# One output-projection tile for all heads, and one Q projection per chunk spread by way of DRAM

## The chip, the cores and the metric

The kernel runs on one core of one Trainium2 chip. The metric is the device time of one launch in microseconds (us). The profile is one execution of the program, recorded by the hardware profiler.

## What is computed

The input `x` has four images of 128 channels and 64 x 64 positions, so 4 x 4096 tokens of 128 channels. Two layers follow each other.

Layer 0 is self-attention with four heads of 32 channels over the 4096 tokens of each image, an output projection, the residual, and a normalisation over channels:

```
Q, K, V = split_heads(x @ Wq + bq), ... (x @ Wk + bk), ... (x @ Wv + bv)
attn = softmax(Q K^T * scale);  out = attn V
y = out @ Wo + bo + x
y = (y - mean) / sqrt(var + eps) * gamma + beta
```

Layer 1 takes that result and adds up three branches: a 3 x 3 convolution, a spectral branch (a channel mix in the Fourier domain, which this kernel rewrites as flips and small matrices), and a state-space branch (Mamba: projection, short convolution, SiLU, a scan over all tokens with 256 channels and 16 states, a gate, a projection).

## The kernel before

**Tiling.** A chunk is 512 tokens (`L`), so there are 32 chunks. A half `H` is one chunk with one pair of heads (`PAIRS` = 2); there are 64 halves. In a half the keys are walked in 32 pieces of 128 (`NT` = 32). The main loop counts steps `t`: step `H * 32 + m` works on piece `m` of half `H`. A chunk is therefore a slot of 64 steps (`SLOT`); below, "position" is the step within its slot.

**What every step does.** `scores_for_exp` (line 480) computes the scores of 128 keys against 512 queries for two heads: per head two matmuls for the high and low parts of Q, and one that subtracts the row maximum (`MX`, `sel`). The Scalar engine (ACT) exponentiates them (line 488). `scores_for_max` (line 436) works `LEAD` = 7 steps ahead for the next half's row maxima, which the Vector engine (DVE) reduces (line 443). `times_values` (line 500) multiplies the exponentials by V and adds up in the PSUM tile `po`; an extra column of ones gives the softmax sum. The two heads of a pair sit at partitions 0 to 32 and 64 to 96.

**The scan.** The state-space scan of an earlier chunk (two slots and 16 steps behind) runs beside that, one scan instruction in every even step: ACT makes the decays (line 801), the GpSimd engine (POOL) the input terms `db` (line 806), DVE scans (line 817), POOL multiplies and accumulates (lines 827 and 846).

**The side jobs.** All the rest is written as Python generators that a small planner, `Plan`, advances while the program is written. Nothing is decided at run time: each engine gets one fixed order. `plan.at(t, rank, job)` says from which step a job may begin. Each `yield` is a wait of at least one step; its letters name what the next piece takes: "P", "D" and "A" are places on TensorE, DVE and ACT, of which there are two each in odd steps and none (one for ACT) in even steps; "B" is one of two PSUM banks. Jobs of a lower rank number go first.

The side jobs that matter here:

- `project_q(H)` runs once per half: one matmul with 512 columns into a bank, then ACT writes the high part and DVE the low part of `Q` (lines 412, 417, 418). The weights hold each head's 32 columns twice, because the rows of `Q` are head 0 twice and head 1 twice (against the high and low parts of K).
- `project_kv` does the same for K, and K's parts already travel through DRAM (`kd`): stored on the SyncE queue (SP) and read back in `place_k`.
- `maxima(H)` turns the row maxima into a tile: POOL widens them (line 452), TensorE transposes (line 459).
- `normalise(H)` runs at positions 1 and 33. It sends the softmax sums through DRAM (`zd`, lines 518 and 521), takes the reciprocal on DVE (line 524), sends it back out (`rd`, line 526), reads it spread over partitions into `r` (line 530), and POOL multiplies the tile `oz[k]` by it (line 533). The tiles `oz[0]` and `oz[1]` have gaps of 32 rows, which hold zeros against zero rows of the projection weights.
- `output_projection(c)`, from position 9: ACT adds `bo` to the residual `xr` (line 548); then, for each of four groups of 128 tokens, two matmuls with `oz[0]` and `oz[1]` and one that adds the transposed residual through the identity matrix (lines 556 and 557), all into `py`; then statistics and the normalised tile `xh` (lines 564 to 587).
- `mamba_input(c)` waits for `xh`; from it come `scan_input`, `scan_bc`, `scan_dt` (which ends in three POOL multiplications, lines 739 to 741, for each of two channel halves), `spectral`, `convolve`, `gate` (lines 757 to 765) and, a slot later, `scan_output`, in which POOL gates the accumulators (line 938) before a projection (line 948).
- `scan_load` (line 784) brings the rows `B` and `C` of the scan over all partitions by DMA into a ring of three buffers, which POOL sets free.

Nearly all DMAs of the loop are issued by SP in one fixed order; a DMA whose data or buffer isn't ready holds up those behind it. The constants are loaded by DMAs that ACT issues before its first computation.

Of the kernel before, what the change touches and what calls it, by code (L numbers as in the profile page):

```python
# [155 lines left out]
def attention_then_conv_mamba(  # L156
# [41 lines left out]
    wat = const.tile([P, 1 + PAIRS, P], F32, name="wat_vo")  # L198
# [9 lines left out]
    Wo = [wat[:, 1 + k, :] for k in range(PAIRS)]  # L208

    wq_t = const.tile([P, PAIRS, 2, 2, HD], F32, name="wq_t")  # L210
    bq = const.tile([P, PAIRS], F32, name="bq")
    for h in range(HEADS):
        k, j = divmod(h, 2)
        c = COL["bq"] + h
        for r in range(2):
            nc.scalar.dma_start(wq_t[:, k, j, r, :], wq[h, :, j * HS : j * HS + HD])
            nc.scalar.dma_start(
                bq[j * HS + r * HD : j * HS + (r + 1) * HD, k : k + 1],
                vecs[j * HS : j * HS + HD, c : c + 1],
            )  # L220
    Wq = [wq_t[:, k].rearrange("c j r d -> c (j r d)") for k in range(PAIRS)]
# [6 lines left out]
    bvk = const.tile([P, PAIRS], F32, name="bvk")  # L228
    nc.vector.memset(wat[:, 1:, :], 0.0)
    nc.vector.memset(bvk, 0.0)  # L230
    for h in range(HEADS):
        row = h % 2 * HS
        hs = slice(h * HD, (h + 1) * HD)
        nc.scalar.dma_start(wat[row : row + HD, 1 + h // 2, :], wvo[1, hs, :])
        nc.scalar.dma_start(
            bvk[row : row + HD, h // 2 : h // 2 + 1], bv[0:1, hs].rearrange("o c -> c o")
        )
# [40 lines left out]
    def constants_of_the_rest():  # L278
# [25 lines left out]
        for k in range(PAIRS):  # L304
            nc.tensor.matmul(pb, Wo[k], bvk[:, k : k + 1], start=k == 0, stop=k == PAIRS - 1)
# [11 lines left out]

    oz = [const.tile([P, L], F32, name=f"oz{k}") for k in range(PAIRS)]
    for k in range(PAIRS):
        nc.gpsimd.memset(oz[k], 0.0)  # L320
# [84 lines left out]
    def project_q(H):  # L405
# [3 lines left out]
        yield ""  # L409
        bank = yield "PB"  # L410
        pq = bank_tile(bank, [P, L], f"pq_{H}")
        nc.tensor.matmul(pq, Wq[k], xqs[c], start=True, stop=True)
        yield "DA"
        plan.release(bank, 2)
        q = att.tile([P, 2, L], F32R, tag="Q", name=f"Q_{H}", bufs=3)
        bias = bq[:, k : k + 1]
        nc.scalar.activation(q[:, 1, :], pq, AF.Identity, bias=bias)
# [94 lines left out]
    def normalise(H, t0):  # L512
# [4 lines left out]
        for j in range(2):  # L517
            nc.sync.dma_start(zd[j : j + 1, :], oz[k][j * HS + HD : j * HS + HD + 1, :])
# [617 lines left out]
```

## Time and profile before

| | |
|---|---|
| median of the runs | 6233.53 us (6230.06 to 6236.76, 3 runs) |
| the profiled execution | 6236.14 us, of which 6234.4 us are its span |
| granted TensorE clock, mean over the span | 0.982 |
| first exponential's matmul starts | about 131 us into the span |
| last step of the main loop ends | about 5984 us |
| TensorE (PE) matmuls busy | 6005.2 us (96%) |
| TensorE weight loads (PEld) busy | 2540.9 us (41%) |
| POOL, DVE, ACT busy | 4579.0 us (73%), 4286.5 us (69%), 3585.0 us (58%) |
| DMA | 405 MB, mean 65 GB/s |

The busy share is of the whole span. Matmuls are pipelined and their ends are modelled, so the distance from one matmul's start to the next says more about TensorE than the length of a row. "Idle before" is the time that an engine stood still ahead of an instruction, and what ended it.

### The profile page before, as it was taken

What the parts mean: (1) busy time and instruction counts of PE and PEld (TensorE: products, weight loads), DVE (VectorE), ACT (ScalarE), POOL (GpSimd) and SP (SyncE); (2) the same over time, 40 slices, a digit from 0 to 9 for tenths busy, and PEclk for the clock granted to TensorE, in tenths of its full rate; (3) what the DMA queues carried; (4) which work ended last, traced back from release to release, by engine and by line L of the source; (5) the groups of instructions that cost most, each with busy time, mean ns of one, the idle gap of its engine ahead of it and who ended that gap; (6) DMA issues with size and microseconds to landing.
All of it is one profiled execution on the core that took longest, in us unless ns stands there. A gap on an engine that the chain in (4) does not pass through costs nothing. (4 is left out here: it accounts for less than half of the span.)

```text
span 6234.4 us, 83338 instructions
## 1 busy us (share of the span) xinstructions
PE 6005.2 (96%) x32076; PEld 2540.9 (41%) x32076; DVE 4286.5 (69%) x4406; ACT 3585.0 (58%) x4858; POOL 4579.0 (73%) x4819
## 2 busy tenths in 40 slices
PE   5999999999999999999999999999999999999966
PEld 2444444444444444444444444444444444444321
DVE  4556776777777676777667777776777666767647
ACT  1455666565666555666656566665566556556643
POOL 0005887778887777888787888777788777778877
PEclk7999999999999999999999999999999999999987
DMA  3001222223222222222322221122322211112223
GB/s 111 14 25 47 63 56 61 63 64 98 79 71 60 63 65 60 62 63 73 89 82 65 61 65 60 57 64 67 98 66 71 55 54 54 54 55 58 63 80 85
DMA packets 234624, 404.97 MB, mean 65 GB/s; under 512 B 39272, under 2 KB 40816, under 8 KB 234224
## 3 DMA queue, kind: packets, MB, share of 16 engines
q1 hardware_dynamic: 229840, 397.75, 22.6%
q8 instruction: 251, 4.11, 0.3%
q10 hardware_dynamic: 4384, 1.89, 0.1%
q14 instruction: 149, 1.22, 0.1%
HBM read 350.54 MB, written 49.02 MB: 64 GB/s over the span
## 5 line engine op out<-in xcount | busy, mean ns | idle before, releaser
L443 DVE TENSOR_REDUCE part<-s 128x2 f32<-128x1024 f32 x2048 | 2501.7, 1222 | 1627.4 <-PE s L436 1625.9
L488 ACT ACTIVATE e<-s 128x1024 f32<-128x1024 f32 x2048 | 2095.5, 1023 | 2271.7 <-PE s L480 2263.0
L500 PE MATMUL po<-e,V 128*33 128x512 f32 x8192 | 2160.9, 606 | 2.6 <-DVE oz L510 0.3
L480 PE MATMUL s<-Q,K 64*128 64x512 f32 x8192 | 1504.7, 445 | 22.3 <-ACT e L488 18.5
L436 PE MATMUL s<-K,Q 64*128 64x512 f32 x8192 | 1322.2, 400 | 41.2 <-DVE part L443 39.6
L827 POOL TENSOR_TENSOR hs<-hs,bc 128x512 f32<-128x512 f32 x952 | 1215.5, 1277 | 177.5 <-DVE hs L817 108.6
L480 PEld LDWEIGHTS s<-Q,K 64*128 64x128 f32 x8192 | 610.7, 185 | 1748.9 <-ACT e L488 1179.0
L806 POOL TENSOR_TENSOR db<-u,bc 128x512 f32<-128x512 f32 x948 | 1214.8, 1281 | 0.0
L846 POOL TENSOR_TENSOR acc<-acc,hs 128x512 f32<-128x512 f32 x900 | 1150.9, 1279 | 70.5
L817 DVE TENSOR_TENSOR_SCAN hs<-dA,state,db 128x512 f32<-128x512 f32 x832 | 1060.7, 1275 | 86.0 <-ACT dA L801 54.0
L436 PEld LDWEIGHTS s<-K,Q 64*128 64x128 f32 x8192 | 766.3, 186 | 276.7 <-DVE part L443 99.4
L480 PE MATMUL s<-MX,sel 64*128 64x512 f32 x4096 | 810.9, 392 | 0.0
L826 POOL COPY state<-hs 128x1 f32<-128x1 f32 x864 | 160.2, 185 | 844.8 <-DVE hs L817 844.8
L801 ACT ACTIVATE dA<-dt,negA 128x512 f32<-128x512 f32 x1024 | 702.6, 686 | 116.0 <-DVE hs L817 63.6
L500 PEld LDWEIGHTS po<-e,V 128*33 128x33 f32 x8192 | 299.3, 109 | 913.8 <-issue 879.7
L480 PEld LDWEIGHTS s<-MX,sel 64*128 64x128 f32 x4096 | 384.6, 185 | 92.6
L891 PE MATMUL pf<-xp,cw 128*128 128x512 f32 x576 | 288.2, 617 | 0.0
L452 POOL COPY wide<-mx 128x128 f32<-128x128 f32 x256 | 63.4, 294 | 200.7 <-DVE mx L449 200.7
L817 DVE TENSOR_TENSOR_SCAN hs<-dA,zero,db 128x512 f32<-128x512 f32 x128 | 163.2, 1275 | 7.7 <-POOL db L806 7.4
L840 PE MATMUL acc<-V,cst 128*128 128x512 f32 x128 | 90.1, 807 | 78.2 <-POOL V L827 78.0
L533 POOL TENSOR_TENSOR oz<-oz,rz 128x512 f32<-128x512 f32 x64 | 81.9, 1280 | 107.1 <-DMA rz<-rd 107.1
L891 PEld LDWEIGHTS pf<-xp,cw 128*128 128x128 f32 x576 | 96.2, 188 | 132.4 <-issue 127.4
(144 smaller groups left out, 3847.8 us busy)
## 6 DMA issues: line engine op xcount, KB each, us to landing
bc<-bcd SPq DMA_DIRECT2D x487, 512.0 KB
K<-kd SPq DMA_DIRECT2D x64, 256.0 KB
rz<-rd SPq DMA_DIRECT2D x128, 128.0 KB
K<-bcd SPq DMA_DIRECT2D x42, 256.0 KB
vd<-vst SPq DMA_DIRECT2D x32, 264.0 KB
V<-vd SPq DMA_DIRECT2D x32, 264.0 KB
xq<-in_x SPq DMA_DIRECT2D x32, 256.0 KB
xk<-in_x SPq DMA_DIRECT2D x32, 256.0 KB
```

The lines of the kernel that those rows point to most:

```text
L436: nc.tensor.matmul(sc[:, j, :], QT[H][rows[j], n, t * P : (t + 1) * P], KK[k][m][rows[j], :], start=n == 0, stop=n == 1,)
L443: nc.vector.tensor_reduce(part[H][:, t, :, m], sc, AX.X, ALU.max)
L480: nc.tensor.matmul(s[:, j, :], sel[rows[j], :] if n == 2 else KK[k][i][rows[j], t * P : (t + 1) * P], mov[rows[j], :], start=n == 0, stop= ...
L488: nc.scalar.activation(e, s, AF.Exp)
L500: nc.tensor.matmul(po[H][used[j], :], VA[i][:, t, 2 * k + j, :], e[:, j, :], start=m == 0, stop=m == NT - 1,)
L801: nc.scalar.activation(dA[c, v], dts[c][hf], AF.Exp, scale=negA[:, k : k + 1])
L806: engine.tensor_tensor(db[c, v], us[c][hf], bcs[c, n][0], ALU.mult)
L817: nc.vector.tensor_tensor_scan(hs, dA.pop((c, v)), db.pop((c, v)), state[:, k : k + 1] if c % NCH else zero, ALU.mult, ALU.add,)
L826: nc.gpsimd.tensor_copy(state[:, k : k + 1], hs[:, L - 1 :])
L827: nc.gpsimd.tensor_tensor(hs, hs, bcs[c, n][1], ALU.mult)
L846: nc.gpsimd.tensor_tensor(accs[c, hf], accs[c, hf], hs, ALU.add)
L891: nc.tensor.matmul(pf, cw[:, k, :], xps[c][:, dy : dy + RPC, dx : dx + W], start=k == 0, stop=False)
```

## The change

Two parts are rearranged.

**Q.** `project_q` runs once per chunk and computes all four heads with one matmul; ACT makes the high and DVE the low part, in the buffers that K's parts use. Both are stored to a DRAM tile `qd`. A new job, `place_q(H)`, reads from it, with four DMAs of 32 rows each, into the rows of `Q` of its half, 8 steps before the half's first row-maximum matmul. The weights and biases of Q are loaded once instead of twice.

**Output projection.** The two heads of a half are copied from `po` to a tile `oz[H]`; from there two more DMAs per half move them, without gaps, to their 32-row places in a tile `sums[c]` that holds all four heads of the chunk. The reciprocals are read into a tile of the same layout. After the second half, POOL multiplies once. `output_projection` is then one matmul with 512 columns and `Wo` as the stationary operand; DVE adds `bo` and the residual in one instruction and writes `xr`; four transposes bring it to the layout in which the statistics are taken. ACT's addition of `bo` is gone. The job starts three steps later and has two more planner stages.

Besides, `maxima` and `scan_output` wait one step more between POOL's work and the matmuls that read it, and the loads of Q's input and the projection of Q are placed earlier.

The diff, cut to its core:

```diff
-    wat = const.tile([P, 1 + PAIRS, P], F32, name="wat_vo")
+    wat = const.tile([P, 2, P], F32, name="wat_vo")
...
-        for r in range(2):
-            nc.scalar.dma_start(wq_t[:, k, j, r, :], wq[h, :, j * HS : j * HS + HD])
-            nc.scalar.dma_start(
-                bq[j * HS + r * HD : j * HS + (r + 1) * HD, k : k + 1],
-                vecs[j * HS : j * HS + HD, c : c + 1],
-            )
-    Wq = [wq_t[:, k].rearrange("c j r d -> c (j r d)") for k in range(PAIRS)]
+        nc.scalar.dma_start(wq_t[:, h, :], wq[h, :, j * HS : j * HS + HD])
+        nc.scalar.dma_start(
+            bq[h * HD : (h + 1) * HD, :], vecs[j * HS : j * HS + HD, c : c + 1]
+        )
+    Wq = wq_t.rearrange("c h d -> c (h d)")
...
-    for h in range(HEADS):
-        row = h % 2 * HS
-        hs = slice(h * HD, (h + 1) * HD)
-        nc.scalar.dma_start(wat[row : row + HD, 1 + h // 2, :], wvo[1, hs, :])
-        nc.scalar.dma_start(
-            bvk[row : row + HD, h // 2 : h // 2 + 1], bv[0:1, hs].rearrange("o c -> c o")
-        )
+    bvc = const.tile([P, 1], F32, name="bvc")
+    nc.scalar.dma_start(Wo, wvo[1])
+    nc.scalar.dma_start(bvc, bv.rearrange("o c -> c o"))
...
-    def project_q(H):
+    def project_q(c):
...
-        nc.tensor.matmul(pq, Wq[k], xqs[c], start=True, stop=True)
+        nc.tensor.matmul(pq, Wq, xqs[c], start=True, stop=True)
         yield "DA"
         plan.release(bank, 2)
+        hi = att.tile([P, L], F32R, tag="khi", name=f"qhi_{c}")
+        lo = att.tile([P, L], F32R, tag="klo", name=f"qlo_{c}")
+        nc.scalar.activation(hi, pq, AF.Identity, bias=bq)
+        nc.vector.scalar_tensor_tensor(lo, pq, bq, hi, ALU.add, ALU.subtract)
+        yield ""
+        qd[c] = dram.tile([2, HEADS, HD, L], F32, tag="qd", name=f"qd_{c}")
+        nc.sync.dma_start(qd[c][0].rearrange("h d l -> (h d) l"), lo.bitcast(F32))
+        nc.sync.dma_start(qd[c][1].rearrange("h d l -> (h d) l"), hi.bitcast(F32))
+
+    def place_q(H):
+        c, k = divmod(H, PAIRS)
+        while c not in qd:
+            yield ""
         q = att.tile([P, 2, L], F32R, tag="Q", name=f"Q_{H}", bufs=3)
-        bias = bq[:, k : k + 1]
-        nc.scalar.activation(q[:, 1, :], pq, AF.Identity, bias=bias)
-        nc.vector.scalar_tensor_tensor(q[:, 0, :], pq, bias, q[:, 1, :], ALU.add, ALU.subtract)
+        for j in range(2):
+            for r in range(2):
+                p0 = j * HS + r * HD
+                nc.sync.dma_start(
+                    q[p0 : p0 + HD].bitcast(F32), qd[c][:, 2 * k + j].rearrange("n d l -> d n l")
+                )
         QT[H] = q
...
# maxima, before its transposes
-        yield ""
-        yield ""
+        for _ in range(3):
+            yield ""
...
# times_values, last piece
-            nc.scalar.activation(oz[k][used[0], :], p[used[0], :], AF.Identity)
-            nc.vector.tensor_copy(oz[k][used[1], :], p[used[1], :])
+            oz[H] = att.tile([P, L], F32, tag="oz", name=f"oz_{H}", bufs=1)
+            nc.scalar.activation(oz[H][used[0], :], p[used[0], :], AF.Identity)
+            nc.vector.tensor_copy(oz[H][used[1], :], p[used[1], :])
...
# normalise
+            nc.sync.dma_start(zd[j : j + 1, :], o[j * HS + HD : j * HS + HD + 1, :])
+        for j in range(2):
+            nc.sync.dma_start(sums[c][head[j], :], o[j * HS : j * HS + HD, :])
...
-            nc.sync.dma_start(r[rows[j], :], rd[j : j + 1, :].to_broadcast([HS, L]))
-        yield ""
-        yield ""
-        nc.gpsimd.tensor_tensor(oz[k], oz[k], r, ALU.mult)
+            nc.sync.dma_start(inverse[c][head[j], :], rd[j : j + 1, :].to_broadcast([HD, L]))
         if k == PAIRS - 1:
-            plan.at(t0, 0, output_projection(H // PAIRS))
+            yield ""
+            yield ""
+            nc.gpsimd.tensor_tensor(sums[c], sums[c], inverse.pop(c), ALU.mult)
+            plan.at(t0, 0, output_projection(c))
...
# output_projection
-        yield "A"
-        nc.scalar.activation(xr, xr, AF.Identity, bias=bo)
+        bank = yield "PB"
+        pa = bank_tile(bank, [P, L], f"pa_{c}")
+        nc.tensor.matmul(pa, Wo, sums.pop(c), start=True, stop=True)
+        yield "D"
+        plan.release(bank, 2)
+        nc.vector.scalar_tensor_tensor(xr, pa, bo, xr, ALU.add, ALU.add)
         bank = yield "PB"
         py = bank_tile(bank, [P, TPC, P], f"py_{c}")
         for t in range(TPC):
-            if t == TPC // 2:
-                yield "P"
-            ts = slice(t * P, (t + 1) * P)
-            for k in range(PAIRS):
-                nc.tensor.matmul(py[:, t, :], oz[k][:, ts], Wo[k], start=k == 0, stop=False)
-            nc.tensor.matmul(py[:, t, :], xr[:, ts], ident, start=False, stop=True)
+            nc.tensor.transpose(py[:, t, :], xr[:, t * P : (t + 1) * P], ident)
...
# scan_output, before its matmuls
-        yield ""
-        yield ""
+        for _ in range(3):
+            yield ""
...
-            plan.at((H - 1) * NT - LEAD - 24, 0, load_q(H // PAIRS))
-        plan.at((H - 1) * NT - LEAD - 14, 0, project_q(H))
+            plan.at((H - 1) * NT - LEAD - 30, 0, load_q(H // PAIRS))
+            plan.at((H - 1) * NT - LEAD - 22, 0, project_q(H // PAIRS))
+        plan.at((H - 1) * NT - LEAD - 8, 0, place_q(H))
         plan.at(H * NT - LEAD, 0, maxima(H))
-        plan.at((H + 1) * NT + 1, 0, normalise(H, (H + 1) * NT + 9))
+        plan.at((H + 1) * NT + 1, 0, normalise(H, (H + 1) * NT + 12))
```

## Prediction

> **What bounds the kernel now.** I read the page first, then windows over single chunks, then TensorE's order of time inside them, and last the waits.
>
> ```profile
> span 6234.4 us, 83338 instructions
> PE 6005.2 (96%) x32076; PEld 2540.9 (41%) x32076; DVE 4286.5 (69%) x4406; ACT 3585.0 (58%) x4858; POOL 4579.0 (73%) x4819
> ```
>
> TensorE's row is full, but matmuls overlap in it, so it only names the suspect. Two whole chunks side by side, one from the middle and one from the last image:
>
> ```profile
> core 0: us, PE busy (x) PEld busy (x) DVE busy (x) ACT busy (x) POOL busy (x), PEclk, DMA share, GB/s
> 2852.64:3036.27 183.63, 182.95 (x1000) 78.16 (x999) 131.54 (x135) 111.43 (x152) 148.04 (x159) 1.00 0.33 95
> 5250.67:5437.70 187.03, 182.45 (x990) 76.20 (x988) 131.08 (x135) 111.38 (x151) 146.82 (x156) 1.00 0.19 55
> ```
>
> The columns after the window are its length and each engine's busy time. The clock is full. TensorE stands still for 0.7 us of 183.6 in the first, for 4.6 us in the second. No other engine is above 81%. Next, TensorE's own order, starts in the first column:
>
> ```profile
> 2879.60 0.73 PE L480 MATMUL s<-Q,K 64*128 64x512 f32 x4
> ...
> 2884.83 0.73 PE L480 MATMUL s<-Q,K 64*128 64x512 f32 x4
> ...
> 2887.17 0.73 PE L480 MATMUL s<-Q,K 64*128 64x512 f32 x4
> ...
> 2888.54 1.12 PE L412 MATMUL pq<-xq,wq_t 128*128 128x512 f32 x2
> ...
> 2890.58 0.73 PE L480 MATMUL s<-Q,K 64*128 64x512 f32 x4
> ...
> 2908.16 0.73 PE L480 MATMUL s<-Q,K 64*128 64x512 f32 x4
> ...
> 2909.53 0.66 PE L638 MATMUL pt<-cst,xh 128*128 128x128 f32 x4
> ...
> 2911.09 0.73 PE L480 MATMUL s<-Q,K 64*128 64x512 f32 x4
> ```
>
> Each L480 row opens a step, so the distance between two of them is a step's price. A bare step, 2884.83 to 2887.17, takes 2.34 to 2.36 us. The step with the output projection, 2879.60 to 2884.83, takes 5.23: the projection costs 2.87. The step with a Q projection, 2887.17 to 2890.58, takes 3.41: that matmul costs 1.06. The step with four transposes, 2908.16 to 2911.09, takes 2.93: they cost 0.57. Side work adds to TensorE's time in full, in odd steps, with nothing of it hidden.
>
> A rule of the Trainium skill speaks against counting on this: "Perfetto Trace Analysis", section "Identifying the Most-Contended Engine", holds matmul busy share to be a poor measure and wants weight-load share instead. That is 41% here, so by the rule TensorE has headroom, taking matmuls off it need not shorten anything, and the PE part of my sum would be nothing, with nothing to give back either: 6236.1 - 12 - 6 - 5, 2.6 less for the median, 6211 us. The step distances show the opposite, and I take them.
>
> **The change part by part.**
>
> *TensorE, per chunk.* Removed: two Q projections (2 x 1.055) and one output projection (2.87), 4.98 us. Added: one Q projection (1.055), the projection `pa`, which is of the same form (1.055), and four transposes of `xr` (0.573, as for `xh`): 2.68 us. The balance is -2.30 us, and over 32 chunks -73.5 us. For the transposes the page "TensorE: Matmul & The Clock Gate", section "Part 4: PE-mode transpose", gives about 275 ns each in a kernel, 1.10 us for four; then the balance would be -57 us. The trace has four of this very shape, at 0.57, and I use that.
>
> *The extra step in `maxima` and `scan_output`.* The waits that these can remove:
>
> ```profile
> PEld s L436 <- DVE part L443: 99.4, 126, 2.0
> PEld pm L459 <- POOL wide L452: 13.4, 35, 0.7
> PEld py L948 <- POOL acc L938: 13.2, 16, 2.6
> ```
>
> (total us, times, longest). One step is 2.35 us, more than the longest 0.7 of the first of POOL's two, so I take -12 of 13.4; of the second, whose waits reach 2.6, half: -6 (bounds 0 and -13). The row maxima come a step later, still some two steps before their first use at position 0 or 32.
>
> *Start.* ACT issues 42 constant DMAs, from 0.76 to 21.9 us, before its first computation at 21.98. Now there are 28 (four fewer for `wq_t` and for `bq`, three fewer for `Wo` and for `bv`). At 0.475 us from one issue to the next that is 6.7 us. Against it stands Q's pair of ACT and DVE instructions ahead of K's, with shared buffers. I take -5 (bounds -7 and +5). The `oz` memsets (1.0 us on POOL) go too; nothing waited for them.
>
> *ACT and DVE.* Per chunk ACT loses one Q part (0.68) and the `bo` addition (0.71). DVE loses one Q part (0.75) and gains the addition from `pa` (about 0.75). ACT is at 61% of a chunk; its loss is worth nothing. DVE's balance is nil. The 99.4 us in which row-maximum matmuls wait for DVE stay as they are; most of them sit at position 2, behind the copy of `po`, which is not touched. The later start (12 for 9) and the extra bank stage delay `xh` by about six steps, 14 us. What is late next is `scan_dt`, some 45 steps on; its last product `u` is finished near position 15, shortly before the scan of its chunk, so some of the planner's gaps between must shrink. I cost that at nothing, with 0 to +20 us in the range.
>
> *SP's queue.* Added per chunk: two stores of Q, eight loads, four moves of heads: 14 issues at about 0.4 us, 5.6 us of a queue that mostly waits. They move past one another thus: at positions 1 and 33 two moves stand ahead of the load of `zc` (+0.8 us for the sum's round trip; the reciprocal at 4 has had no idle time before it); at 17 and 49 four loads of Q follow `scan_load`, and K's loads and `wr` queue behind them (1.6 us, needed much later). Cover for `place_q` is eight steps, at position 17 about 21 us (steps of 2.34 with a gate, a transposition and a projection among them). The nearest rows: the rd to rz round trip holds SP 126.3 us in 64 waits, 2.0 us each; the slowest store in sight, `vd` in the crowded start, was issued at 28.91 and set ACT free at 39.8, 11 us. A load of 128 KB then lands 4 to 13 us after SP reaches it; either fits, so nothing. The moves of heads, SBUF to SBUF, have no row; 2 to 11 us by the same two, against five steps (12 us) before POOL needs them: nothing, +10 us at worst.
>
> *POOL.* One multiplication of 1.28 us per chunk goes, at position 39, where POOL has time. It does not go where POOL has none:
>
> ```profile
> 2893.89 1.28 POOL L827 TENSOR_TENSOR hs<-hs,bc 128x512 f32<-128x512 f32 x1
> 2895.24 1.29 POOL L846 TENSOR_TENSOR acc<-acc,hs 128x512 f32<-128x512 f32 x1
> 2896.49 1.27 POOL L806 TENSOR_TENSOR db<-u,bc 128x512 f32<-128x512 f32 x1
> ...
> 2897.99 1.27 DVE L817 TENSOR_TENSOR_SCAN hs<-dA,state,db 128x512 f32<-128x512 f32 x1
> ```
>
> From position 5 to 17 POOL runs without a gap: two bare steps give it 4.70 us, the scan takes 4.02 of them (3 x 1.28 and 0.18), and the six products of `scan_dt`, the gates and the last `oz` product come on top. TensorE's 2.87 and 1.06 us of side work in that stretch are what lets POOL keep up; the `db` above ends at 2897.76 and the scan that needs it starts 0.23 us later. Behind that scan on DVE stands the next row-maximum reduction, and for that TensorE waits. After the change the stretch holds one Q projection and `pa`, 2.11 us instead of 3.93, so 1.8 us less. Take off 0.23 and about 0.5 of slack on DVE, and 1.0 us per chunk comes back as a wait, in the 30 slots with a scan: +30 us. Bounds: 0 (if `scan_dt` falls beside other side work), and what the last image's chunks lose in their own first 46 us, where `scan_dt` falls in bare steps: 4.0 us by the windows, against 0.6 in the middle chunk, so +100.
>
> *Sum.* -73.5 - 12 - 6 - 5 + 30 = -66.5 against the profiled execution's 6236.1 (span 6234.4); that execution is 2.6 us above the median, so 6167 us. The tail after the last step (250 us) I leave as it is: `pa`, addition and transposes there (1.7, 0.75, 0.8) replace 5.3 us of `py`, and the wait of 18.3 us for the last `oz` stays; 5 us either way.
>
> **The rivals.**
>
> *Nothing is given back* (chance 0.25). `scan_dt` comes later and falls beside `pa`, the transposes and the gate's matmul. Then -96.5: 6137 us. For it: 19% of POOL is free over a chunk. Against it: the 0.23 us.
>
> *Most is given back* (0.19). POOL's and DVE's lag grows as in the last image, by some 2.7 us per chunk, 80 us: 6217 us. For it: the 187.03 us chunk, which lacks a K and V projection (2.1 us) and is still 3.4 us longer. Against it: `scan_dt` should come later, not earlier, than there.
>
> *Q arrives late* (0.08), the slower side. The loads of Q stand in SP's order behind `scan_load`, whose wait for POOL is SP's longest item (4041.6 us in 476 waits, the longest 37.0). If SP stood there for most of the 21 us, the first row-maximum matmul, and everything behind it on TensorE, would wait in each half. From 1.04 us per half on (66.5 / 64) the gain is gone; at 1.8 us it would be +115: 6282 us. Against it: at position 17 SP issued its `bc` load at 2899.28, one microsecond into the step.
>
> **How the numbers follow.** The likeliest case (0.48) spans 6150 to 6190 by its bounds. The range, 6122 to 6224, reaches to the first rival's lower end and takes in most of the second; outside are the third and the tails, about 0.18. This kernel's measurement can tell 0.2%, 12.5 us, from no change. Faster by more than that: 0.48 + 0.25 + two thirds of 0.19 = 0.86; within: 0.06; slower: 0.08.
>
> **What would show it.** Right: a middle chunk of about 182 us; steps with `pq` or `pa` at 3.4 us, with four `xr` transposes at 2.93; the wait of `pm` for `wide` near zero; 32 fewer POOL products; ACT's first computation near 15 us; more DVE scans waiting for POOL's `db`, with bare steps above 2.4 us near position 17. Wrong: waits of L436 for a DMA of Q (third rival); chunks still at 183 us with TensorE idle for 2 us or more in each (second); chunks below 181 us (first).

## The result and the profile after

The changed kernel takes 6134.17 us (median of 5 runs, 6132.92 to 6136.61) against 6233.53: a ratio of 0.984, 95% interval [0.9829, 0.9851], 99 us less. The prediction was 6167 us with 6122 to 6224 as its range; the direction and the range held, the middle was 33 us too high.

The page of the changed kernel, its span and the busy time of each engine:

```profile
span 6134.7 us, 82692 instructions
PE 5914.9 (96%) x31434; PEld 2454.4 (40%) x31434; DVE 4291.6 (70%) x4404; ACT 3557.2 (58%) x4794; POOL 4534.8 (74%) x4785
```

POOL has 34 instructions fewer. TensorE's share is the same 96% as before, which again says nothing about where the 99 us went. One chunk from the middle and one from the last image, as before (window and length, then the engines' busy time, the granted TensorE clock and the DMA columns):

```profile
2812.62:2994.45 181.83, 180.81 (x980) 75.56 (x978) 131.58 (x135) 110.90 (x150) 146.66 (x158) 1.00 0.37 104
5179.02:5359.67 180.65, 179.11 (x971) 74.17 (x970) 131.23 (x134) 109.58 (x148) 145.44 (x156) 1.00 0.24 65
```

The middle chunk lost 1.8 us (183.63 before). The chunk of the last image lost 6.4 (187.03 before); it had been the longer of the two and is now the shorter, as it should be, since it has no K and V projection (2.1 us). That second loss is what the prediction's sum did not hold.

TensorE's order of time in that middle chunk, three steps with the new side work (start, length, operation). As before, the distance from one `s<-Q,K` row to the next is the price of a step:

```profile
2825.53 0.73 PE L483 MATMUL s<-Q,K 64*128 64x512 f32 x4
...
2826.90 1.13 PE L397 MATMUL pq<-xq,wq_t 128*128 128x512 f32 x2
...
2828.94 0.73 PE L483 MATMUL s<-Q,K 64*128 64x512 f32 x4
```

```profile
2846.46 0.73 PE L483 MATMUL s<-Q,K 64*128 64x512 f32 x4
...
2847.84 1.13 PE L562 MATMUL pa<-op,wat_vo 128*128 128x512 f32 x2
...
2849.88 0.50 PE L483 MATMUL s<-Q,K 64*128 64x512 f32 x2
```

```profile
2856.93 0.73 PE L483 MATMUL s<-Q,K 64*128 64x512 f32 x4
...
2858.28 0.66 PE L569 MATMUL py<-cst,xr 128*128 128x128 f32 x4
...
2859.85 0.74 PE L483 MATMUL s<-Q,K 64*128 64x512 f32 x4
```

The steps take 3.41, 3.42 and 2.92 us; a bare one takes 2.35. So Q's projection and `pa` cost 1.06 us each and the four transposes 0.57, the prices of the prediction. The waits that it named, and two new ones, in the changed kernel (total us, times, longest):

```profile
PEld s L439 <- DVE part L446: 77.1, 125, 2.0
DVE hs L829 <- POOL db L818: 43.2, 57, 3.6
PEld s L483 <- DVE MX L470: 38.6, 29, 1.6
PE s L483 <- DVE MX L470: 25.9, 29, 1.1
```

Loads of weights for `pm` waited 13.4 us for `wide` before and wait 0.4 us now, and the second layer's `py` no longer waits for POOL's gate product. The wait for the row-maximum reduction on DVE fell from 99.4 to 77.1 us. DVE's scans wait for POOL's `db` more often, as forecast: 57 times, against 18 times before:

```profile
DVE hs L817 <- POOL db L806: 32.0, 18, 3.5
```

The last two lines of the view above are new. The tile of row maxima is late once per chunk, at position 32:

```profile
2897.32 0.74 PE L483 MATMUL s<-Q,K 64*128 64x512 f32 x4
2898.94 0.50 PE L483 MATMUL s<-MX,sel 64*128 64x512 f32 x2 [0.88 <-DVE MX L470]
```

Where the span's 99.7 us went, from the start of each chunk's first step in the two traces:

| stretch | before, us | after, us | difference | per chunk |
|---|---|---|---|---|
| up to the first exponential's matmul | 131.4 | 127.4 | -3.9 | |
| chunks 0 and 1 | 326.8 | 323.1 | -3.6 | -1.8 |
| chunks 2 and 3 | 369.6 | 359.9 | -9.7 | -4.9 |
| chunks 4 to 25 | 4050.2 | 4007.3 | -42.9 | -1.95 |
| chunks 26 to 30 | 934.0 | 903.4 | -30.6 | -6.1 |
| chunk 31 to its last step's start | 171.6 | 166.2 | -5.4 | -5.4 |
| after that | 250.9 | 247.5 | -3.4 | |

### The profile page after: what moved, and what is told of

Read it like the earlier page. It is cut to its first block, busy times and chain, and to the rows that moved or that the text cites. A ratio compares the mean times of both kernels' runs of the same rounds, so it can differ in the third digit from the quotient of the medians.

```text
span 6134.7 us, 82692 instructions
## 1 busy us (share of the span) xinstructions
PE 5914.9 (96%) x31434; PEld 2454.4 (40%) x31434; DVE 4291.6 (70%) x4404; ACT 3557.2 (58%) x4794; POOL 4534.8 (74%) x4785
## 5 line engine op out<-in xcount | busy, mean ns | idle before, releaser
L439 PEld LDWEIGHTS s<-K,Q 64*128 64x128 f32 x8192 | 762.0, 185 | 255.2 <-DVE part L446 77.1
L701 POOL TENSOR_TENSOR xs<-xs,sg_x 128x512 f32<-128x512 f32 x64 | 82.4, 1287 | 59.1 <-ACT sg_x L625 59.1
```

The costliest lines, as they stand in the source:

```text
L439: nc.tensor.matmul(sc[:, j, :], QT[H][rows[j], n, t * P : (t + 1) * P], KK[k][m][rows[j], :], start=n == 0, stop=n == 1,)
```

## The experiments

The theory on trial: TensorE's prices hold, so its saving is 2.30 us per chunk; what a kernel gains beyond or short of that depends on where the planner then puts POOL's side products against the scan and against the matmuls that read them. The rival: the removed work and the removed waits are worth a fixed amount each, wherever the rest stands. Each kernel was timed in alternation with the kernel before, whose medians there were 6231 to 6234.5 us.

From here on, a chunk or a position without a number is a mean: of chunks 4 to 25 for the middle chunks, of chunks 26 to 30 for the last image. "In the written order" means the step in which the planner hands an instruction to its engine; an engine that is behind runs it some steps later.

### One part at a time

The kernel before with the Q part alone:

```diff
-    def project_q(H):
+    def project_q(c):
...
+    def place_q(H):
...
-            plan.at((H - 1) * NT - LEAD - 24, 0, load_q(H // PAIRS))
-        plan.at((H - 1) * NT - LEAD - 14, 0, project_q(H))
+            plan.at((H - 1) * NT - LEAD - 30, 0, load_q(H // PAIRS))
+            plan.at((H - 1) * NT - LEAD - 22, 0, project_q(H // PAIRS))
+        plan.at((H - 1) * NT - LEAD - 8, 0, place_q(H))
```

> The kernel before with the Q part of the change alone (one Q projection per chunk, its parts stored to qd and placed 8 steps ahead; eight constant DMAs fewer); output projection, its position 9 and the two-step waits as before. Theory A (each matmul taken off TensorE is paid back in full, and the parts add up): one 1.06 us projection less in each of 32 chunks is -34 us, and eight ACT issues of 0.475 us less at the start is -4, so about 38 us below the kernel before, ratio 0.994. Theory B (most of the 99 us comes from where the side jobs fall, not from TensorE's work): the last image's chunks, 187 us each in the kernel before, may move by several us, either way, so the total leaves -38 by more than 10.

Measured: 6275.03 us, 1.0061 [1.0045, 1.0078]. It is slower by 40 us with 34 us less on TensorE. Its middle chunks take 187.7 us (184.1 before). With Q's second projection gone, both halves of `scan_dt` come due together, and in the written order POOL gets all six of its products at position 1 (three at 5 and three at 11 before). It runs them in the steps at positions 3 to 5. POOL's rows in chunk 15 (start, length), and below them two of DVE and one of TensorE:

```profile
2898.80 1.27 POOL L754 TENSOR_TENSOR spe<-u,spe 128x512 f32<-128x512 f32 x1
2900.16 1.29 POOL L755 TENSOR_TENSOR dt<-dt,spe 128x512 f32<-128x512 f32 x1
2901.52 1.27 POOL L756 TENSOR_TENSOR u<-dt,xs 128x512 f32<-128x512 f32 x1
2902.75 1.29 POOL L754 TENSOR_TENSOR spe<-u,spe 128x512 f32<-128x512 f32 x1
2904.12 1.28 POOL L755 TENSOR_TENSOR dt<-dt,spe 128x512 f32<-128x512 f32 x1
2905.48 1.29 POOL L756 TENSOR_TENSOR u<-dt,xs 128x512 f32<-128x512 f32 x1
...
2909.57 1.27 POOL L821 TENSOR_TENSOR db<-u,bc 128x512 f32<-128x512 f32 x1
```

```profile
2910.87 1.28 DVE L832 TENSOR_TENSOR_SCAN hs<-dA,state,db 128x512 f32<-128x512 f32 x1 [2.46 <-POOL db L821]
2912.07 1.20 DVE L458 TENSOR_REDUCE part<-s 128x2 f32<-128x1024 f32 x1
...
2913.33 0.73 PE L451 MATMUL s<-K,Q 64*128 64x512 f32 x4 [0.48 <-DVE part L458]
```

Read from the top: 8 us of products hold up `db`; the DVE scan stands 2.46 us for `db`; the reduction queued behind that scan starts late; TensorE waits for it. Positions 6, 8 and 10 take 2.74, 3.19 and 3.17 us and not 2.38, 2.39 and 2.48 as before. This is the mechanism of the prediction's POOL step, at twice its price, but not in the changed kernel. It is 1.9 us of some 5 us of new waits in a middle chunk: the rest stands at position 15 (0.9, a wait for DVE's reduction), 21 (1.2, a wait for POOL's gate product) and 33 to 35 (1.0, DVE's reduction again). In the last image the same edit parts the six products, three at 61 and three at 5: positions 6, 8 and 10 fall from 3.78, 3.04 and 3.19 us to 2.35, 2.45 and 2.48, and the chunk from 186.8 to 182.3.

The kernel before with the projection part alone:

```diff
-        nc.gpsimd.tensor_tensor(oz[k], oz[k], r, ALU.mult)
...
+            nc.gpsimd.tensor_tensor(sums[c], sums[c], inverse.pop(c), ALU.mult)
...
+        nc.tensor.matmul(pa, Wo, sums.pop(c), start=True, stop=True)
...
-        plan.at((H + 1) * NT + 1, 0, normalise(H, (H + 1) * NT + 9))
+        plan.at((H + 1) * NT + 1, 0, normalise(H, (H + 1) * NT + 12))
```

> The kernel before with the output-projection part alone (all heads moved into one tile, one long matmul, addition on DVE, four transposes, start at position 12; six constant DMAs fewer); Q as before, two-step waits as before. Theory A: 2.87 - 1.06 - 0.57 = 1.24 us per chunk, -40 us, and -3 at the start: 43 us below the kernel before. Theory B: since this part also starts the chain towards the next scan some six steps later, the last image's chunks lose their stalls as well (187 to about 182 us, five or six chunks, -25 to -30): about 70 us below the kernel before.

Measured: 6172.6 us, 0.9899 [0.9884, 0.9914]: 61 us less, of which TensorE's balance is 40 (1.24 us per chunk). This lies between the two theories. Middle chunks take 183.4 us, those of the last image 181.3 (186.8 before). All of the surplus is in the last image: 5.5 us per chunk there, 1.1 in chunks 2 to 25. There the written order gives POOL the six products at 5 and 9 and no longer all at 1, and positions 6, 8 and 10 take 2.38, 2.34 and 2.48 us.

The kernel before with its projection started later and nothing else:

```diff
-        plan.at((H + 1) * NT + 1, 0, normalise(H, (H + 1) * NT + 9))
+        plan.at((H + 1) * NT + 1, 0, normalise(H, (H + 1) * NT + 15))
```

> The kernel before with one number changed: the output projection may start at position 15 instead of 9, so that the chain behind it comes about six steps later, as in the changed kernel; no work is removed. Theory A (the last image's stalls go because TensorE, ACT and POOL have less to do): the last image's chunks stay near 187 us and the time within 10 us of the kernel before. Theory B (they go because scan_dt's six POOL products no longer fall in bare steps): the last image's chunks come down to 182 to 183 us and the kernel gains about 25 to 30 us, middle chunks unchanged at 183.6.

Measured: 6302.04 us, 1.0105 [1.009, 1.012], slower by 68; neither theory had that. In the last image the edit doesn't move the six products, which stay at position 1 with 3.76, 3.03 and 3.19 us at 6, 8 and 10, so theory B isn't tested by it. In the middle chunks the projection's 2.87 us of matmuls stood at position 11, beside POOL's busy stretch, and lengthened its steps. Moved to 17, they leave bare steps there, and positions 14 to 16 stretch by 2.4 us together. In chunk 14 TensorE waits 2.73 us for an exponential of ACT; ahead of it on ACT stands an instruction that waits 3.34 us for POOL's gate product `zg`. So a start that is only later is not what helped.

The changed kernel with its projection started where it was before:

```diff
-        plan.at((H + 1) * NT + 1, 0, normalise(H, (H + 1) * NT + 12))
+        plan.at((H + 1) * NT + 1, 0, normalise(H, (H + 1) * NT + 9))
```

> The changed kernel with one number set back: the output projection may start at position 9 instead of 12. By the written order the middle chunks keep scan_dt's products in two places (1 and 9), but the last image's chunks get all six at position 1, as the kernel before had them. Theory C: the last image's chunks go from 180.7 to 184 to 186 us, six or seven of them, +20 to +35 us; middle chunks within 1 us. Rival (the last image gains because TensorE has less to do): last image's chunks stay near 181, time within 10 us of the changed kernel.

Measured: 6314.81 us, 1.0132 [1.0117, 1.0147], 181 us above the changed kernel, far above both theories. TensorE's wait for the sums, a single one of 21.3 us in the changed kernel, is here (total us, times, longest):

```profile
PE pa L562 <- POOL op L547: 129.9, 30, 22.1
```

In its middle chunks the step with `pa`, position 9, takes 8.3 us and not 3.4: POOL's product of the sums stands behind the scan's products and `scan_dt`'s. In the changed kernel the matmul stands at position 13, and in the loop it waits for nothing. The later start belongs to the one long matmul.

### Is it POOL?

The Q part alone, with `scan_dt` started four steps later, so that its six products split:

```diff
-            plan.now(1, scan_dt(c, hf, xd))
+            plan.at(plan.t + 4, 1, scan_dt(c, hf, xd))
```

> The Q part alone, as in e1, with one edit: scan_dt may begin four steps after scan_bc instead of at once. By the written order that moves the six POOL products of scan_dt in a middle chunk from one place (all six at position 1) to two places (three at position 3, three at 9); the last image's chunks keep theirs, three at 61 and three at 5. Theory C (e1 lost its gain because both halves of scan_dt fell on POOL together, in bare steps): middle chunks fall from 188.0 us to 182 to 184, and the kernel from 1.006 of the kernel before to 0.993 to 0.997, that is, the 34 us of TensorE work come out. Rival D (it is the place of the Q projection, or SP's extra DMAs, which are as in e1): no more than 10 us below e1.

Measured: 6245.17 us, 1.0018 [1.0009, 1.0027], 30 less than the Q part alone. That is more than rival D allows and less than theory C had (6190 to 6215). Positions 6, 8 and 10 go back to 2.35, 2.44 and 2.53 us, as C says. Positions 15 and 21 get somewhat worse (3.62 and 5.91 us, from 3.22 and 5.51).

The Q part alone, in the same order of work, without two of the three products of each half (this leaves out both subtractions of `scan_dt`, so its step sizes are other numbers):

```diff
-        nc.gpsimd.tensor_tensor(e, w, e, ALU.subtract)
-        nc.gpsimd.tensor_tensor(z, z, e, ALU.subtract)
```

> The Q part alone, as in e1, with two of scan_dt's three POOL products left out in each half (spe and the subtraction from dt; the step sizes dt are then not quite softplus). Order and places are those of e1; POOL has 4 x 1.28 us less in each chunk, at the place where six stood together; TensorE, DVE and ACT keep all they have. Theory C (POOL is what TensorE waits for there): most of the 4 to 5 us per chunk go, 30 chunks, so 100 us or more below e1. Rival E (ACT's and DVE's part of scan_dt, or the scan's own order on DVE, holds TensorE): under 30 us below e1.

Measured: 6227.01 us, 0.9988 [0.998, 0.9997], 48 less than the Q part alone. Neither number came (100 or more, less than 30). Positions 6, 8 and 10 take 2.35, 2.35 and 2.45 us. Nothing but work on POOL was taken away, so the 2.0 us per chunk at these positions were POOL's. Positions 15 (3.20) and 21 (5.51) do not move: those are other waits, which theory C had counted in.

### The third steps

The changed kernel with `maxima` back at two steps:

```diff
 # maxima, before its transposes
-        for _ in range(3):
-            yield ""
+        yield ""
+        yield ""
```

> The changed kernel with the wait in maxima set back from three steps to two. Theory A: the third step makes the tile of row maxima late in each half at position 32 (that step takes 3.49 us in the changed kernel, 25.9 us of TensorE waits for MX in 29 halves), so going back removes about 26 us and brings back at most the 13 us of waits for the widened maxima: 13 to 26 us below the changed kernel. Rival: the maxima tile is late for another reason (its bank is given late), then the waits for MX stay and 0 to 13 us come on top.

Measured: 6122.3 us, 0.9816 [0.9802, 0.9831]. It beats both kernels, the changed one by 12 us. Position 32 falls from 3.49 to 2.67 us; loads of weights for `pm` wait for `wide` again, 20.0 us in 39 waits (0.4 in the changed kernel). In this order of work the third step costs more than it saves. It is not alone in that: position 32 still stands 0.3 us over a bare step, so a part of the rival holds too, as the next experiment shows.

The changed kernel with `scan_output` back at two steps:

```diff
 # scan_output, before its matmuls
-        for _ in range(3):
-            yield ""
+        yield ""
+        yield ""
```

> The changed kernel with scan_output back at two steps, all else kept: its matmul goes from position 23 to 21, four steps after POOL gets the gate product. Theory A (the third step takes a wait away, as the prediction's -12 and -6 said it would): position 21 is 5.5 us and not 4.27, 32 x 1.26 = +40, so 6174; at the prediction's size (0.19 us a chunk) 6140. Theory B (in the changed kernel POOL is in time at position 21 too, since its sums products stand elsewhere): 6128 to 6140, position 21 at 4.3.

Measured: 6206.75 us, 0.9958 [0.9944, 0.9973]: 73 us above the changed kernel, well over what either theory gave the step. Position 21 takes 7.1 us in the middle chunks, where its work is worth 4.27. In chunk 15, POOL's gate product, then TensorE:

```profile
2896.37 2.48 POOL L950 TENSOR_TENSOR acc<-acc,zg 128x512 f32<-128x512 f32 x2
```

```profile
2894.22 0.73 PE L483 MATMUL s<-Q,K 64*128 64x512 f32 x4
...
2897.68 3.55 PE L960 MATMUL py<-acc,outw 128*128 128x512 f32 x4 [2.02 <-POOL acc L950]
...
2902.14 0.50 PE L483 MATMUL s<-Q,K 64*128 64x512 f32 x2
```

TensorE stands 2.02 us for the first of two products and stretches the matmuls over the second: this step takes 7.92 us. The same two rows in the changed kernel:

```profile
2869.04 2.51 POOL L950 TENSOR_TENSOR acc<-acc,zg 128x512 f32<-128x512 f32 x2
```

```profile
2873.02 1.98 PE L960 MATMUL py<-acc,outw 128*128 128x512 f32 x4
```

POOL ends at 2871.55, TensorE comes at 2873.02 and waits for nothing. POOL is no faster; the matmul stands two positions later. The matmuls of position 21 there would have come at about 2868.3 (the step starts at 2866.92, side work 1.37 us into it) and would have waited until 2870.3, the end of the first product, as they do here; that is an estimate. In the last image of this experiment, the planner also put the six `scan_dt` products together, and positions 6, 8 and 10 take 2.71, 3.03 and 3.21 us there. By whole chunks the loss is 2.3 us, in chunks 2 to 25 as in the last image, for position 32 gives 1.15 us back: it takes 2.34 us here, with the third step of `maxima` in place. With `scan_output`'s matmul at position 21 a bank is free two steps sooner, POOL widens the maxima at position 27 and not at 29, and the tile is in time. So the late tile of the changed kernel has two causes, the third step of `maxima` and the bank that `scan_output`'s third step holds longer.

Both back at two steps:

```diff
 # maxima and scan_output, in each
-        for _ in range(3):
-            yield ""
+        yield ""
+        yield ""
```

> The changed kernel with maxima and scan_output both at two steps: the one long matmul and the single Q projection as they are. The maxima's third step cost 12 us (e4). The planner then also puts POOL's six scan_dt products of a last-image chunk together at position 1. Theory A (the third step of scan_output is needed, and six products in a row cost 2 us a chunk as in e1): 6134 - 12 + 40 + 5 x 2 = 6172. Theory B (the removed PE work is all there is): 6122 to 6130.

Measured: 6168.14 us, 0.9897 [0.9882, 0.9912]. Theory A's number, but not by its parts: position 21 takes 4.77 us here, 0.5 over its work and not 3. Another 1.1 us per chunk are at positions 33 to 37, where two multiplications of the convolution stand ahead of a row-maximum reduction on DVE. Taking a step away in one job has moved others.

The kernel before with the Q part and both third steps:

```diff
 # the Q part as above; maxima and scan_output, in each
-        yield ""
-        yield ""
+        for _ in range(3):
+            yield ""
```

> The Q part alone (as e1) with both third steps of the change added: scan_output's matmul then stands at position 23 of a chunk and not 21, the maxima's turn goes to 28. In e1 (6275) position 21 took 5.53 us where its work is priced at 4.27, and POOL's six products at position 1 cost 2.05 us at positions 6 to 10; they stay there. Theory A (the gate product on POOL is what position 21 waited for; moving away from it pays): position 23 takes 4.27, some 24 middle chunks x 1.26 = -30, the maxima's third step gives up to 10 back: 6245 to 6255. Theory B (POOL is behind by a fixed amount of work, so the wait only turns up at another position): 6265 or more, with a new step that is over its price by about as much.

Measured: 6253.62 us, 1.0033 [1.0021, 1.0046], 21 us less than the Q part alone, as theory A had it. The step with the second layer's output matmuls, now at position 23, takes 4.27 us; positions 8 and 10 stay at 3.2.

The changed kernel without its Q part:

```diff
-    def project_q(c):
+    def project_q(H):
...
-            plan.at((H - 1) * NT - LEAD - 30, 0, load_q(H // PAIRS))
-            plan.at((H - 1) * NT - LEAD - 22, 0, project_q(H // PAIRS))
-        plan.at((H - 1) * NT - LEAD - 8, 0, place_q(H))
+            plan.at((H - 1) * NT - LEAD - 24, 0, load_q(H // PAIRS))
+        plan.at((H - 1) * NT - LEAD - 14, 0, project_q(H))
```

> The changed kernel without its Q part: one long projection and both third steps, but Q projected once for each half as before. Added back is one 1.055 us projection a chunk, 34 us. By itself the Q part made the kernel before 40 us slower (e1). Theory A (what the Q part is worth depends on where it lets the planner put POOL's work; beside the other parts the places are good and its TensorE price holds or more): 6168 to 6190. Theory B (the Q part costs in any company, through its two copies by DRAM and its earlier start): 6134 or less. With the projection alone and two steps at 6172.6 (e2), and the maxima's third step at 12, the sum of parts would be 6185.

Measured: 6151.42 us, 0.9869 [0.9852, 0.9885]. This is below theory A's bounds and above B's. The two third steps are worth 21 us here (against the projection alone, 6172.6) and 34 in the changed kernel (against both at two steps); the Q part then brings 17 of TensorE's 34. The 21 us are those of `maxima`: `scan_output`'s matmuls stand at position 25 in both kernels. With the projection alone `pm` waits for `wide`,

```profile
PE pm L446 <- POOL wide L439: 21.4, 26, 1.6
```

and positions 29 (where it stands) and 30 take 7.3 us together. Here it stands at 30, one wait of 0.8 us is left, the two positions take 5.9 us, and position 32 takes 2.45. The step that costs 12 us in the changed kernel gains 21 in this one.

### How late Q may be placed

The changed kernel with two steps between `place_q` and Q's first use, not eight:

```diff
-        plan.at((H - 1) * NT - LEAD - 8, 0, place_q(H))
+        plan.at((H - 1) * NT - LEAD - 2, 0, place_q(H))
```

> The changed kernel with Q placed 2 steps ahead of its first use instead of 8, about 5 us instead of 21; all else in the same order. The prediction's two bounds for the landing after SP reaches the loads were 4 and 13 us (four issues of 0.4 us included). If 4: nothing, within 5 us of the changed kernel. If 13: TensorE waits some 8 us for Q in each half and loses part of that, 300 us or more slower. What lies between gives the landing time: the wait per half is the landing less about 5 us.

Measured: 6599.01 us, 1.0588 [1.0573, 1.0604], 465 us above the changed kernel, 7.3 us per half. One of the waits in its chunk 15, first SP's issue of a `bc` load and of the four loads of Q, then TensorE:

```profile
3086.47 0.37 SPq L796 DMA_DIRECT2D bc<-bcd  x1
3086.89 1.87 SPq L419 DMA_DIRECT2D Q<-qd  x4
```

```profile
3094.47 2.00 PE L439 MATMUL s<-K,Q 64*128 64x512 f32 x4 [8.19 <-DMA Q<-qd]
3096.40 1.92 PE L503 MATMUL po<-e,V 128*33 128x512 f32 x4
3098.25 1.22 PE L483 MATMUL s<-Q,K 64*128 64x512 f32 x4
```

Q is there 7.6 us after SP begins to issue. The loads were due in the step that starts at 3078.68, but SP stood 10.7 us at the `bc` load ahead of them, waiting for POOL to set its buffer free, and issued them when TensorE had been waiting for 0.6 us. This is the mechanism of the prediction's third rival. In the changed kernel SP issued the loads of the same half at 2859.36, within the step at position 17, and the first matmul that needs them follows in the step at 2878.27 (position 25). With the 7.6 us of this experiment that leaves about 12 us to spare, an estimate; the trace of the changed kernel has no wait of TensorE for Q.

## Why the prediction came out as it did

**TensorE, -73.5.** The prices were right: 1.06, 1.06 and 0.57 us in the three steps above. The rule that the prediction set aside (the Trainium skill, "Perfetto Trace Analysis", section "Identifying the Most-Contended Engine") names two measures of TensorE's headroom, the share of peak arithmetic and the share of weight loads. The prediction had taken the second alone; by itself PEld's 41% would be room to spare, and the result speaks against that here. The first was not worked out. For the transposes the prediction multiplied a duration. The Trainium skill ("TensorE: Matmul & The Clock Gate", section "Part 4: PE-mode transpose") gives about 275 ns for one of bf16 in one kernel, and an f32 transpose lasts about that here (the maxima's, in the changed kernel: count, total busy us, mean ns of one):

```profile
L462 PE MATMUL pm<-cst,wide 128*128 128x128 f32 x256 | 42.4, 289 | 0.0
```

But four of them overlap, and add 0.57 us to a step, not 1.1.

The prices hold for work that is alone in its step; work in company costs less. The two `pdt` matmuls took one step of 4.27 us at position 63 before, so 1.92 us together; now they stand apart and cost 1.05 each. The transposes of the second row maxima cost 0.39 us beside convolution matmuls (a step of 4.65 us, and 4.26 without them), and 0.58 alone at position 60 now. So a middle chunk has 1.9 us less work on TensorE in the new order, not 2.30.

**The middle chunks, by errors that cancel.** By the prediction's terms a chunk gains 2.30 + 18/32 - 30/32 = 1.93 us on average. Chunks 4 to 25 gained 1.95. That the two agree is luck. TensorE's term was 0.4 too large, as just said, and three others were wrong:

- *POOL gives back 1.0 us per chunk.* It did not. Bare steps near position 17 stayed at 2.35 but for position 16 (2.44 before, 2.54 after), position 21 stands 0.2 over a bare step, and positions 6 and 10 take 0.16 less together. More scans wait for `db`, but the steps there do not lengthen. The step that failed took `scan_dt` to stay inside the stretch while the side work left it, 2.11 us of 3.93. In chunk 15 the steps at 5 to 17 have 3.75 us of side work: `pq` at 5, a gate's matmul at 9 and `pa` at 13 (1.06 each), and the transposes of `xr` at 17 (0.57); with the gate's matmul at 17 they had 4.99 before. And the planner put half of the products at position 1, ahead of the stretch and beside a `pdt` matmul that stands there now, and half at 9, behind the gate's matmul. Which of the two kept the wait away is not shown. That the forecast mechanism exists is shown by the Q part alone: with all six at position 1 it cost 1.9 us per chunk.
- *The third step of `maxima`, -12.* The wait of `pm` went, as said. "Still some two steps before their first use" was wrong: once per chunk the tile is late at position 32, by 1.14 us, and going back to two steps made the kernel 12 us faster. The prediction counted the wait that a step takes away, and not the slack that it uses up at the other end. Nor did it see that POOL's widening itself would come two steps later, at position 29 and not at 27, for want of a bank; where it stays at 27, as with `scan_output` back at two steps, the third step makes nothing late.
- *The waits for DVE stay as they are.* Position 2, where most of them sat, fell from 3.10 to 2.39 us in the middle chunks, and the waits at 0 and 30 by 0.3 each: a `pdt` matmul now stands in the step before position 2, and the maxima's transposes at 30 and not at 27. In all fourteen traces position 2 takes 2.35 to 2.4 us where position 1 has side work, and 3.1 to 3.2 where it has none.

**The third step of `scan_output`, -6.** Read from a trace in which, in the written order of the middle chunks, TensorE's matmuls stood at position 31, five behind POOL's gate product at 26, so that nearly nothing waited. In the changed order the product stands at 18 and the matmuls three positions behind it with two steps, five with three. Taking the step back costs 73 us there, by the experiment, the jobs that move with it included. It was a large part of the gain rather than a small addition to it; not all of it, since with both third steps taken back 65 of the 99 us are left.

**Where the other 33 us came from.** Chunks 2 and 3 and 26 to 31 gained 45.7 us; at the predicted 1.93 us each it would have been 15.4. That is 30 of the 33; the tail has the rest. Chunk 3 and those of the last image had, before, what the Q part alone has in its middle chunks: six `scan_dt` products in bare steps. Of the 6.1 us per chunk of the last image, TensorE's work in its new company is 2.5; 2.8 are the stalls at positions 6, 8 and 10 (3.78, 3.04 and 3.19 us before; 2.35, 2.45 and 2.44 after), 0.9 the one at 15, 1.0 those at 33 to 35, 0.6 those at 21 and 30; the maxima's late tile takes 1.1 back, and position 27 another 0.4 (these parts add up to 6.3). The prediction saw these stalls, in the 187.03 us chunk, and used them as an upper bound of the loss. It did not ask whether the change would take them away: there the products now stand at 3 and 9. Where an experiment on the changed kernel puts all six back at position 1 (`scan_output` at two steps, alone or with `maxima`), the last image has 2.7, 3.0 and 3.2 us at 6, 8 and 10 again. This is the term the sum lacked.

**Start, -5, and tail, 0.** -3.9 and -3.4. The first exponential's matmul starts between 124.5 and 128.6 us in kernels with this start, so these two are right in kind and no finer. ACT's first computation starts at 15.7 us, as forecast.

**The rivals.** The number of "nothing is given back" (6137) came true, by another way than it said: the middle chunks stand at 182 us, not below 181. "Most is given back" happened, and more, when the Q part stood alone, for the reason given for it in less than half. "Q arrives late" has about 12 us in hand.

**How the parts add up.** They don't:

| kernel | us | step |
|---|---|---|
| before | 6233.5 | |
| with the projection part | 6172.6 | -61 (TensorE -40) |
| and both third steps | 6151.4 | -21 |
| and the Q part: the changed kernel | 6134.2 | -17 (TensorE -34) |
| the third step of `maxima` taken back | 6122.3 | -12 |

The Q part is worth -17 at the end of this row and +40 at its beginning, and the third step of `maxima` +12 at the end and -21 beside the projection part. Shown is that POOL's six products in a row make the stalls at positions 6 to 10 of the Q part alone (products left out); in all fourteen traces those at 6 and 8 stand just where the six are together at position 1. Shown are also that TensorE waits for the gate product (rows), and that moving one job by a step moves others. Open is which of the planner's choices sets the place of each; no rule was found that gives the position of `scan_dt` from an edit without writing out the order.

## What to carry to other kernels

Where an engine's order is fixed at build time and TensorE is full, the price of a removed matmul can be read from the distance between two steps. It held to a few hundredths of a us for work alone in its step; two matmuls in one step cost 1.92 us and not 2.11. The gain is that price plus whatever the new order does to the engine in second place. Write out the new order for every kind of chunk and look, at each hand-over from the second engine, how many steps lie between producer and reader, before a wait or a stall is booked as kept or removed. A spare step between producer and reader has no fixed worth: one was worth 73 us in this kernel, and another gained 21 us or cost 12, by what stood around it.

## What the runs showed of the hardware

A long stop of TensorE costs more than the stop. In the experiment with late loads of Q, windows around the 8.19 us wait (window and length, engines, granted clock, DMA):

```profile
3080.00:3086.00 6.00, 6.00 (x30) 2.31 (x28) 3.90 (x4) 2.43 (x3) 5.51 (x10) 1.00 0.01 2
3086.00:3094.00 8.00, 0.27 (x4) 0.00 (x0) 0.84 (x1) 1.61 (x2) 6.80 (x7) 0.83 0.73 152
3094.00:3098.00 4.00, 3.49 (x8) 0.98 (x8) 1.50 (x3) 0.00 (x0) 0.00 (x0) 0.50 0.07 24
3098.00:3102.00 4.00, 4.00 (x16) 1.67 (x14) 2.81 (x7) 1.02 (x1) 1.43 (x2) 0.57 0.00 0
3102.00:3106.00 4.00, 4.00 (x28) 2.29 (x28) 2.56 (x4) 1.60 (x2) 2.57 (x3) 1.00 0.01 4
```

The clock is full before the wait, 0.50 and 0.57 in the two windows of 4 us after TensorE resumes, and full again: `s<-Q,K` takes 1.22 us there and not 0.73, `po` 1.92 and not 1.05. The two steps take 12.95 and 3.77 us where bare ones take 2.35, so the stop of 8.2 us cost 12.0. That the clock halves after at least one idle window of some 3.4 us is what the Trainium skill states ("TensorE: Matmul & The Clock Gate", section "Part 1: The HAM clock gate (the "warmup" mystery)"); here it fell some 5 us into the stop (0.83 over 8 us leaves 2.7 us at half). The page has the clock back after at least one busy window of the same length, and here it took about 7 us (0.57 over 4 us leaves half a microsecond of full clock). In the changed kernel, whose waits in the loop are about a microsecond, the windows of both chunks have a clock of 1.00. In the experiment with the early projection, the mean clock over the span fell from 0.986 to 0.972.

The four loads of Q, 512 KB by the profile's count in rows of 2 KB, landed within 8 us of SP's first issue, with the `bc` load of 512 KB issued just ahead of them.
